# Softplus of an edge written as exponential and logarithm alone, with a bound on its argument found on the chip

## The chip, the cores and the metric

The kernel runs on one core of a Trainium2 chip. The time is that of the core from launch to the end of the program, in microseconds (us); of several runs the median counts. The engines are called as the profile calls them: PE (TensorE, with PEld for its weight loads), DVE (VectorE), ACT (ScalarE), POOL (GpSimd) and SP (SyncE, which here issues most DMAs).

## The reference

One layer of message passing on a graph of 6250 nodes and 200000 edges, 128 features. Of the nodes, h = relu(layernorm(x)) is multiplied by a weight matrix. An edge e goes from `dst[e]` to `src[e]` in the sense below; it has 20 attributes f in [0, 1) and a weight c in [0, 1):

```python
def shifted_softplus(x):
    return jax.nn.softplus(x) - LOG2

x = atomic_embedding @ W_in                              # h @ W_in
W_ij = shifted_softplus(f_ij @ W_f1 + b_f1) @ W_f2 + b_f2
W_ij = W_ij * f_ij_cutoff
x_ij = x[idx_j] * W_ij                                   # idx_j = dst
out = jax.ops.segment_sum(x_ij, idx_i, num_segments=N_ATOMS)   # idx_i = src
return shifted_softplus(out @ W_o1 + b_o1) @ W_o2 + b_o2
```

`W_f1` is 20x128, drawn from a normal distribution and divided by the root of 20; `b_f1` has a spread of 0.1. The argument of the edge's softplus is z = f @ W_f1 + b_f1. The result is added to the layer's input.

## The kernel before

**The edge work.** The edges stand in chunks of 128; 1563 chunks make 391 quads of four. One step i of the main loop works on several quads at once, each at another stage, and the order of every engine is written out by hand (`manual_schedule`): each step runs a fixed list of functions, and between them hooks put there beforehand by `at(step, point, function)`. The points are named after their engines (`D0`, `D1`, `DM`, `D2` for DVE, `A0` to `A2` for ACT, `PE2`, `L` for loads, `S` for scatters).

For a quad q the stages are:

- `s1_pe` (L309): z, a matmul of the attributes (split into three bf16 parts, 123 rows) into a PSUM bank of tag A. It is issued one step ahead.
- `s1_exp` and `s1_ln` on ACT: e = |z| (L314), e = exp(-e) (L315), e = ln(0.5 e + 0.5) (L320), each over 128x512.
- `s1_guard` on DVE (L485): a = max(z, 0) + e. This is softplus(z) - log 2.
- in the next step `s2_pe_x` and `s2_pe_w` on PE: the gathered node rows xg (L500, one-hot products), and W = b2 + a @ W_f2 (L497, L508, f32).
- `s2_copy` on ACT (L513): xc = xg times the edge weight, four instructions; `s2_m` on DVE (L523): the message m = W * xc.

**Where the messages go.** There are three ways. 168 quads are *sorted*: their messages are split into bf16 parts (L679), permuted into slots by products with one-hots (L665, L690), copied out by ACT (`mst`, L696), and later summed into the transposed accumulator `accT` by the *units*: 96 small products at a time (L784) into four PSUM banks, which DVE adds up (L795). What overflows the slots goes through L705 to L749 (`po`, `osum`, `os`) and a scatter. 192 quads are *listed*: their unsummed messages are scattered straight to DRAM by POOL, one instruction for each chunk (`scatter`, L585, an indirect DMA with addition), with duplicates sent to a dense list that is added later. 31 quads are plain: duplicates of a chunk are summed by a product (L535), and then scattered. There are four accumulators in DRAM, taken in turn.

**Tiles.** Four PSUM banks carry tag A (z, xg and W in turn), four tag B (all other products). The SBUF tags of the change: "e" with 2 buffers (e), "a" with 2 buffers (a; at the start also the first weights, `w1f`). Message tiles "s" have 4 buffers.

**Beside it.** The 49 blocks of attributes are split into bf16 parts 4096 edges at a time (`fb_1` to `fb_4`, L267 to L280, one block in eight steps), the node rows are prepared in 25 groups up to the middle of the loop (`prep_*`), and ranks for the sorted quads are counted in 21 groups (L596 to L654).

**The end.** What the fast path can't treat (an edge outside of its window, an overflow) is marked. A flag is computed and read into a register of every engine (L1233), and a loop over all chunks (L1234) runs as often as the flag says: 0 times, or once for each chunk. With a count of 0 all engines pass its branches, and its end waits for the landings of all DMAs. Then the tail loads the accumulators (L1309), sums them (L1315, L1321), and applies the output layers.

Of the kernel before, what the change touches and what calls it, by code (L numbers as in the profile page):

```python
# [7 lines left out]
F32 = mybir.dt.float32  # L8
BF16 = mybir.dt.bfloat16
# [11 lines left out]
P = 128  # L21
# [25 lines left out]
NACC = 4  # L47
FPARTS = ((0, 3), (3, 2), (5, 1))
CQ = 16
EARLY_N = 256  # L50


@with_exitstack
def tile_gnn(ctx: ExitStack, tc: tile.TileContext, x, fB, cT, srcT, srcr, dstr, win_, wf1, wf2, bias, bo1c, wo1,
# [64 lines left out]
    dropd = dp.tile([P, EP // P], BF16, name="dropd")  # L119

    con = cp.tile([P, 16], F32, name="con")
    loads = {}
    st = {}
    fst = {}
# [143 lines left out]
        fst[b]["f3"] = f3  # L268

    def fb_2(b):  # L270
        fr = wk.tile([P, FE], F32, tag="fr", name="fr", bufs=1)
        nc.vector.tensor_tensor(fr, fst[b]["f"], fst[b]["f3"][:, 0], op=ALU.subtract)
        fst[b]["fr"] = fr
# [36 lines left out]
        st.setdefault(q, {})["z"] = z  # L310

    def s1_exp(q):
        e = wk.tile([P, 512], F32, tag="e", name="e")
        nc.scalar.activation(e, st[q]["z"], AF.Abs)  # L314
        nc.scalar.activation(e, e, AF.Exp, scale=-1.0)  # L315
        st[q]["e"] = e

    def s1_ln(q):
        e = st[q]["e"]
        nc.scalar.activation(e, e, AF.Ln, bias=half, scale=0.5)  # L320
        st[q]["l"] = e

    def s1_oh(q):
        if q % 2 == 0:
# [151 lines left out]
    def l_ji(j):  # L476
# [2 lines left out]
        nc.vector.scalar_tensor_tensor(jd[:, 1:2], mp["L", j]["os"][:, P:P + 1], wgt2, jd[:, 0:1], op0=ALU.is_lt,  # L479
                                       op1=ALU.mult)  # L480
        mp["L", j]["jd"] = jd

    def s1_guard(q):
        a = wk.tile([P, 512], F32, tag="a", name="a")
        nc.vector.scalar_tensor_tensor(a, st[q]["z"], 0.0, st[q]["l"], op0=ALU.max, op1=ALU.add)  # L485
        st[q]["a"] = a

    def nchunks(q):
        return min(4, NCH - 4 * q)
# [349 lines left out]
    with tc.manual_schedule():  # L839
# [36 lines left out]
        nc.vector.tensor_scalar(thr, iot[:, 1:GRP], float(GN), None, op0=ALU.mult)  # L876

        def split3(dst, src, rows, c0, tag):
            p = wk.tile([rows, 3, P], BF16, tag="e", name=f"{tag}_parts")
            r = wk.tile([rows, P], F32, tag="xc", name=f"{tag}_rem")  # L880
            nc.vector.tensor_copy(p[:, 0], src)
            nc.vector.tensor_tensor(r, src, p[:, 0], op=ALU.subtract)
            nc.vector.tensor_copy(p[:, 1], r)
            nc.vector.tensor_tensor(p[:, 2], r, p[:, 1], op=ALU.subtract)
            nc.vector.tensor_scalar(dst, p[:, 0], con[:rows, c0:c0 + 1], None, op0=ALU.mult)
            for k in range(1, 3):
                nc.vector.scalar_tensor_tensor(dst, p[:, k], con[:rows, c0 + k:c0 + k + 1], dst, op0=ALU.mult,
                                               op1=ALU.add)
# [145 lines left out]
        def late_add():  # L1034
            nc.vector.tensor_tensor(bo2b, bo2b, late["bps"][:, 0], op=ALU.add)

        def r0_load(g):
            o, T = tgroups[g]
            t_ = ld.tile([P, 4, P], F32, tag="fb", name="r0t", bufs=2)
            nc.sync.dma_start(t_[:, :T], accs[0][o:o + T * P, :].rearrange("(t p) f -> p t f", p=P))  # L1040
            pst["r", g] = t_
# [14 lines left out]
        def x_bias(t):  # L1056
# [2 lines left out]
            nc.vector.tensor_tensor(v, v, bo2b.unsqueeze(1).to_broadcast([P, n, P]),  # L1059
                                    op=ALU.add)  # L1060

        at(mid, "L", late_loads)
        at(mid + 6 if spread else 0, "PE2", late_bias)
        at(mid + 7 if spread else 0, "D0", late_add)
# [104 lines left out]
        for i in range(max(NQ + 7, last + 16, r0_end + 2, lend + 24)):  # L1169
            if i % 2 == 0 and i // 2 + 2 <= (NQ - 1) // 2:  # L1170
                load_sc(i // 2 + 2)
            run(i, "L")
            run(i, "D0")
            if i < NQ:
                s1_oh(i)
            run(i, "D1")
            if 0 <= i - 1 < NQ:
                s1_eq(i - 1)
            if 0 <= i - 1 < NQ:
                s2_pe_x(i - 1)  # L1180
                s2_pe_w(i - 1)
            if i + 1 < NQ:
                s1_pe(i + 1)
            if i < NQ:
                s1_exp(i)
                s1_ln(i)
            if 0 <= i - 3 < NQ and not full[i - 1]:
                s3_copy(i - 3, 0)
                s3_copy(i - 3, 1)
            run(i, "A0")  # L1190
            if 0 <= i - 4 < NQ:
                s3_ji(i - 4)
            run(i, "A1")
            if 0 <= i - 1 < NQ:
                s2_copy(i - 1)
            if i < NQ:
                s1_guard(i)
            run(i, "DM")
            if 0 <= i - 1 < NQ:
                s2_m(i - 1)  # L1200
            if 0 <= i - 3 < NQ:
                s3_idx(i - 3)
            full[i] = sum(fn in banked for fn, _ in hooks.get((i, "PE2"), [])) > 2
            if 0 <= i - 2 < NQ:
                s3_pe(i - 2)
                if full[i]:
                    s3_copy(i - 2, 0)
                    s3_copy(i - 2, 1)
            run(i, "PE2")
            run(i, "A2")  # L1210
            run(i, "D2")
            if 0 <= i - 4 < NQ and plainq(i - 4):
                s3_scatter(i - 4)
            if 0 <= i - 2 < NQ and i - 2 not in mpi and not plainq(i - 2):
                s3_scatter(i - 2)
            run(i, "S")
# [10 lines left out]
    nc.tensor.matmul(fps[:, 6:7], onesc, dmax, start=True, stop=True)  # L1227
    flag1 = cp.tile([1, 1], F32, name="flag1")
    nc.vector.tensor_reduce(flag1, fps[:, 0:7], axis=AX.X, op=ALU.max)
    flagi = cp.tile([1, 1], I32, name="flagi")  # L1230
    nc.vector.tensor_scalar(flagi, flag1, 0.0, float(NCH), op0=ALU.is_gt, op1=ALU.mult)

    trips = nc.values_load(flagi, min_val=0, max_val=NCH, skip_runtime_bounds_check_because="0 or the number of chunks")  # L1233
    with tc.For_i(0, trips, 1) as ci:  # L1234
        dcol = wk.tile([P, 1], I32, bufs=1, tag="dcol", name="dcol")
        nc.sync.dma_start(dcol, dstr.rearrange("s (e o) -> (s e) o", o=1)[bass.ds(ci * P, P), :])
# [27 lines left out]
        nc.vector.tensor_scalar(ok[:, 0:1], rcol, float(WIN), None, op0=ALU.is_ge)  # L1264
        nc.vector.tensor_scalar(ok[:, 1:2], rcol, 0.0, None, op0=ALU.is_lt)
        nc.vector.tensor_tensor(ok[:, 2:3], ok[:, 0:1], ok[:, 1:2], op=ALU.add)
        nc.vector.scalar_tensor_tensor(ok[:, 3:4], ok[:, 2:3], xcol, ccol, op0=ALU.max, op1=ALU.mult)
        xw = wk.tile([P, P], F32, bufs=1, tag="rm", name="fxw")
        nc.vector.tensor_tensor(xw, x3[:, 0], x3[:, 1], op=ALU.add)
        nc.vector.tensor_tensor(xw, xw, x3[:, 2], op=ALU.add)  # L1270
        z = ps.tile([P, P], F32, tag="A", name="fz", bufs=4)
        nc.tensor.matmul(z, ws, ft[:K1, :], start=True, stop=True)
        e = wk.tile([P, P], F32, tag="e", name="fe")
        nc.scalar.activation(e, z, AF.Abs)
        nc.scalar.activation(e, e, AF.Exp, scale=-1.0)
        nc.scalar.activation(e, e, AF.Ln, bias=half, scale=0.5)
# [189 lines left out]
def _layout(inputs):  # L1466
    import numpy as np

    p = "L0_gnn_"
    x = np.asarray(inputs["x"])  # L1470
    src, dst = np.asarray(inputs["src"]), np.asarray(inputs["dst"])
    f, c = np.asarray(inputs["edge_attr_20"]), np.asarray(inputs["edge_weight1"])
    n, e = x.shape[0], src.shape[0]
    rb = f.shape[1]
    be = 4 * SC
    np_ = -(-n // P) * P
    ep = -(-e // be) * be
    pad = ep - e
    xp = np.pad(x, ((0, np_ - n), (0, 0)))
    fp = np.pad(f, ((0, pad), (0, 0)))  # L1480
    srcp = np.concatenate([src, (np.arange(pad) * (n // P) % n).astype(src.dtype)])
    dstp = np.pad(dst, (0, pad), mode="edge")
    n_sc = ep // SC
    caps = np.array(base_caps(np_, n_sc), np.float32)
    lane = np.arange(P)
    con = np.zeros((P, 16), np.float32)
    con[:, 0] = lane % HB // 3
    con[:, 1] = np.power(3.0, 63.0 - lane)
    con[:, 2] = 2.0 * con[:, 1]
    con[:, 3] = np_ + lane  # L1490
    con[:, 4] = 0.5
    con[:, 13] = lane
    con[:, 14] = np_ // GRP // 2 - con[:, 3]
    nch = -(-e // P)
    nq = -(-nch // 4)
    mq = sorted_quads(nq)
    order = [q for q in range(nq) if q not in mq] + mq + list(range(nq, ep // P // 4))
    cols = np.array([4 * q + c for q in order for c in range(4)])
    cmap = np.empty(ep // P, np.int32)
    cmap[cols] = np.arange(ep // P)  # L1500
    con[:n_sc // 2, 5] = caps[:n_sc // 2]
    con[:n_sc // 2, 6] = caps[n_sc // 2:]
    part = np.array([0, 0, 0, 1, 1, 2])
    for r in range(6 * rb + 3):
        con[r, 7 + (part[r // rb] if r < 6 * rb else r - 6 * rb)] = 1.0
    for r in range(3):
# [40 lines left out]
```

## Time and profile before

| | us |
|---|---|
| median of 3 runs (2149.01 to 2157.57) | 2155.19 |
| the profiled execution | 2165.61 |
| its span, first to last instruction | 2162.8 |
| mean granted PE clock | 0.963 |

The profile is one execution. Its page gives the busy time of each engine, and further views split it: by stretches of time (busy time of PE, PEld, DVE, ACT and POOL with the number of instructions in brackets, the granted clock, the mean busy share of the DMA engines and GB/s), by groups of instructions (line, engine, operation, output<-inputs, shape, count, then busy time, mean duration in ns, and the idle time of the engine just before, with what ended it), and by waits (who waited for what: total us, times, longest). In a timeline a row is the start, the length, the engine, the line, the operation, and in brackets the idle time before it. "issue" is idle time in which the engine waited for nothing that the profile shows.

The main loop runs from about 25 us (the first z) to about 2093 us; the last scatter starts at 2103.61 us and the first load of the tail at 2107.71 us.

### The profile page before, as it was taken

What the parts mean: (1) busy time and instruction counts of PE and PEld (TensorE: products, weight loads), DVE (VectorE), ACT (ScalarE), POOL (GpSimd) and SP (SyncE); (2) the same over time, 40 slices, a digit from 0 to 9 for tenths busy, and PEclk for the clock granted to TensorE, in tenths of its full rate; (3) what the DMA queues carried; (4) which work ended last, traced back from release to release, by engine and by line L of the source; (5) the groups of instructions that cost most, each with busy time, mean ns of one, the idle gap of its engine ahead of it and who ended that gap; (6) DMA issues with size and microseconds to landing.
All of it is one profiled execution on the core that took longest, in us unless ns stands there. A gap on an engine that the chain in (4) does not pass through costs nothing.

```text
span 2162.8 us, 58140 instructions
## 1 busy us (share of the span) xinstructions
PE 1889.9 (87%) x20377; PEld 1314.9 (61%) x20377; DVE 1846.0 (85%) x4782; ACT 1707.1 (79%) x4473; POOL 1635.6 (76%) x1040
## 2 busy tenths in 40 slices
PE   3578998988999899899999999899999999999966
PEld 2456665666666666566666666566666666666744
DVE  4689897997998999898989979989898898898845
ACT  3579887987887888788789878888888889888814
POOL 3678787877777777777777778878887888867674
PEclk8699999999999999999999999999999999999988
DMA  6887666766666666666666656666665666656648
GB/s 243 219 205 144 104 125 106 129 120 116 120 109 119 117 121 123 112 118 114 114 118 123 113 107 120 107 115 121 116 126 100 125 117 106 112 111 115 127 47 238
DMA packets 381191, 272.58 MB, mean 126 GB/s; under 512 B 97727, under 2 KB 341354, under 8 KB 380898
## 3 DMA queue, kind: packets, MB, share of 16 engines
q0 software_dynamic: 143728, 71.30, 33.0%
q1 hardware_dynamic: 236882, 197.50, 31.9%
q8 instruction: 160, 2.62, 0.5%
q14 instruction: 133, 1.09, 0.2%
q10 hardware_dynamic: 288, 0.07, 0.0%
HBM read 154.45 MB, written 114.24 MB: 124 GB/s over the span
## 4 chain that ended last, share of the span: by engine, by line
PE 44%; DVE 22%; ACT 17%; DMA 6%; issue 6%; POOL 3%; SPq 2%; DVEq 0%; ACTq 0%; POOLq 0%
PE pq L690 12%; PE un L784 11%; PE W L508 9%; ACT xc L513 4%; ACT e L315 3%; ACT e L314 3%; POOL acc L585 2%; DMA acc<-s,ji 2%; ACT mst L696 2%; DVE pm L665 2%; DVE eql L367 2%; DVE a L485 2%; DVE pt L679 2%; ACT e L320 2%; DVE accT L795 2%
## 5 line engine op out<-in xcount | busy, mean ns | idle before, releaser
L585 POOL DMA_INDIRECT acc<-s,lji x768 | 1238.7, 1613 | 343.1 <-issue 179.7
L690 PE MATMUL pq<-pt,pm 128*128 128x387 bf16 x2688 | 535.7, 342 | 48.2 <-DVE pt L679 23.0
L513 ACT ACTIVATE xc<-xg,cb 128x128 f32<-128x128 f32 x1564 | 446.0, 372 | 62.8 <-PE xg L500 54.8
L508 PE MATMUL W<-w,a 128*128 128x128 f32 x3128 | 466.4, 294 | 0.2 <-DVE a L485 0.2
L784 PE MATMUL un<-so,mst 32*128 32x392 bf16 x8064 | 385.5, 328 | 43.4 <-ACT os L749 27.1
L508 PEld LDWEIGHTS W<-w,a 128*128 128x128 f32 x3128 | 390.5, 196 | 42.5 <-issue 2.9
L690 PEld LDWEIGHTS <-pm 128*128 128x128 bf16 x2688 | 259.9, 99 | 242.1 <-issue 32.0
L696 ACT CAST mst<-pq 128x387 bf16<-128x387 f32 x672 | 297.9, 481 | 114.8 <-PE pq L690 82.4
L784 PEld LDWEIGHTS <-mst 32*128 32x128 bf16 x8064 | 250.0, 94 | 173.0 <-issue 92.6
L485 DVE SCALAR_TENSOR_TENSOR a<-z,e 128x512 f32<-128x512 f32 x391 | 266.2, 681 | 49.5 <-ACT e L320 41.9
L320 ACT ACTIVATE e<-e,con 128x512 f32<-128x512 f32 x391 | 282.3, 722 | 12.7
L585 POOL DMA_INDIRECT acc<-s,ji x123 | 201.5, 1638 | 99.3 <-ACT ji L566 43.5
L314 ACT ACTIVATE e<-z 128x512 f32<-128x512 f32 x391 | 239.7, 613 | 28.6 <-PE z L309 20.5
L315 ACT ACTIVATE e<-e 128x512 f32<-128x512 f32 x391 | 246.4, 630 | 12.4
L679 DVE TENSOR_TENSOR pt<-pt 128x512 f32<-128x512 f32 x336 | 231.8, 690 | 5.8
L665 DVE TENSOR_SCALAR pm<-iot,pos 128x576 bf16<-128x576 f16 x672 | 219.4, 387 | 0.0
L795 DVE TENSOR_TENSOR accT<-un,accT 128x392 f32<-128x392 f32 x320 | 158.7, 557 | 64.0 <-PE un L784 29.5
L769 DVE TENSOR_SCALAR so<-iot,mst 128x392 bf16<-128x392 f16 x672 | 188.6, 341 | 5.8 <-PE un L784 5.8
L309 PE MATMUL z<-ft,ws 123*128 123x512 bf16 x391 | 152.1, 390 | 32.1 <-DMA ft<-fsd 14.8
L585 POOL DMA_INDIRECT acc<-os,oji x96 | 154.0, 1604 | 31.1 <-issue 14.3
L523 DVE TENSOR_TENSOR s<-W,xc 128x512 f32<-128x512 f32 x192 | 131.5, 685 | 50.3 <-ACT xc L513 39.1
L500 PE MATMUL xg<-wn,oh 63*128 63x128 bf16 x1564 | 157.1, 222 | 13.4 <-DVE a L485 5.9
(197 smaller groups left out, 2662.0 us busy)
## 6 DMA issues: line engine op xcount, KB each, us to landing
rb<-reld SPq DMA_DIRECT2D x391, 64.0 KB
fsd<-f SPq DMA_DIRECT2D x49, 480.0 KB
ft<-fsd SPq DMA_DIRECT2D x195, 120.0 KB
sb<-src SPq DMA_DIRECT2D x169, 128.0 KB
fb<-in_fB_dram SPq DMA_DIRECT2D x49, 320.0 KB
ft<-fsd SPq DMA_DIRECT2D x195, 80.0 KB
wn<-tab SPq DMA_DIRECT2D x782, 15.8 KB
acc<-s,lji POOLq DMA_INDIRECT x768
```

The lines of the kernel that those rows point to most:

```text
L314: nc.scalar.activation(e, st[q]["z"], AF.Abs)
L315: nc.scalar.activation(e, e, AF.Exp, scale=-1.0)
L320: nc.scalar.activation(e, e, AF.Ln, bias=half, scale=0.5)
L485: nc.vector.scalar_tensor_tensor(a, st[q]["z"], 0.0, st[q]["l"], op0=ALU.max, op1=ALU.add)
L508: nc.tensor.matmul(W[:, c, :], st[q]["a"][:, c * P:(c + 1) * P], w2, start=False, stop=(c == 3))
L513: nc.scalar.mul(xc[:, c, :], st[q]["xg"][:, c, :], late["c", q // CQ][:, 4 * (q % CQ) + c:4 * (q % CQ) + c + 1])
L585: nc.gpsimd.indirect_dma_start(out=accs[k][:rows, :], out_offset=bass.IndirectOffsetOnAxis(ap=ji, axis=0), in_=s, in_offset=None, compute_ ...
L665: nc.vector.tensor_scalar(pm[:, c], iot[:, :SLOTS], rk[r]["pos"][:, 4 * j + c:4 * j + c + 1], None, op0=ALU.is_equal)
L679: nc.vector.tensor_tensor(pt[:, :, k * P:(k + 1) * P], a, high(a), op=ALU.subtract)
L690: nc.tensor.matmul(t[:, :PW], mp[q]["pm"][:, c, s * P:(s + 1) * P], high(mp[q]["pt"][:, c:c + 1, :PW])[:, 0], start=(c == 0), stop=(c == 3))
L696: nc.scalar.copy(mp[q]["ms", s][:, :PW], mp[q].pop(("q", s))[:, :PW])
L784: nc.tensor.matmul(ts[g][:, :GN], mp[q]["ms", s][v, k * P:(k + 1) * P], mp[q]["oh"][v], start=(q == qs[0] and k == 0), stop=(q == qs[-1] a ...
```

## The change

The softplus of an edge is computed as ln(0.5 exp(z) + 0.5), without |z| and without max(z, 0): Abs on ACT and the guard on DVE are left out, and the product with W_f2 reads what ACT wrote. This is right as long as exp(z) stays in range. So a bound on |z| is found on the chip: the largest magnitude of the attributes (one reduction for each of the 49 blocks, in `fb_2`) or 1, times the largest column sum of |W_f1| and |b_f1|. If it is over 60, a new loop before the old one clears the accumulators, and the old one treats every chunk, with the old formula.

```diff
+ZMAX = 60.0
...
+    fmax = cp.tile([P, NB], F32, name="fmax")
+    zcol = cp.tile([P, 4], F32, name="zcol")
...
     def fb_2(b):
+        nc.vector.tensor_reduce(fmax[:, b:b + 1], fst[b]["f"], axis=AX.X, op=ALU.max, apply_absolute_value=True)
...
     def s1_exp(q):
-        e = wk.tile([P, 512], F32, tag="e", name="e")
-        nc.scalar.activation(e, st[q]["z"], AF.Abs)
-        nc.scalar.activation(e, e, AF.Exp, scale=-1.0)
-        st[q]["e"] = e
+        a = wk.tile([P, 512], F32, tag="e", name="a", bufs=3)
+        nc.scalar.activation(a, st[q]["z"], AF.Exp)
+        st[q]["a"] = a
 
     def s1_ln(q):
-        e = st[q]["e"]
-        nc.scalar.activation(e, e, AF.Ln, bias=half, scale=0.5)
-        st[q]["l"] = e
+        a = st[q]["a"]
+        nc.scalar.activation(a, a, AF.Ln, bias=half, scale=0.5)
...
-    def s1_guard(q):
-        a = wk.tile([P, 512], F32, tag="a", name="a")
-        nc.vector.scalar_tensor_tensor(a, st[q]["z"], 0.0, st[q]["l"], op0=ALU.max, op1=ALU.add)
-        st[q]["a"] = a
...
+        def bound_abs():
+            t_ = wk.tile([K1, P], F32, tag="h", name="wabs", bufs=1)
+            nc.scalar.activation(t_, w1f, AF.Abs)
+            v_ = wk.tile([K1, P], F32, tag="rm", name="wsel", bufs=1)
+            nc.vector.tensor_copy(v_, con[:K1, 15:16].to_broadcast([K1, P]))
...
+        def bound_sum():
+            t_ = ps.tile([P, 512], F32, tag="B", name="gps", bufs=4)
+            nc.tensor.matmul(t_[:, :P], late["wabs"][1], late["wabs"][0], start=True, stop=True)
...
+        def bound_max():
+            nc.vector.tensor_reduce(zcol[:, 0:1], late["gps"][:, :P], axis=AX.X, op=ALU.max)
+
+        def large_own():
+            nc.vector.tensor_reduce(zcol[:, 1:2], fmax, axis=AX.X, op=ALU.max)
+            nc.vector.scalar_tensor_tensor(zcol[:, 1:2], zcol[:, 1:2], 1.0, zcol[:, 0:1], op0=ALU.max, op1=ALU.mult)
+            nc.vector.tensor_scalar(zcol[:, 2:3], zcol[:, 1:2], ZMAX, None, op0=ALU.is_gt)
+
+        def large_any():
+            t_ = ps.tile([P, 512], F32, tag="B", name="lps", bufs=4)
+            nc.tensor.matmul(t_[:, 0:1], onesf, zcol[:, 2:3], start=True, stop=True)
...
+        def large_all():
+            nc.vector.tensor_scalar(zcol[:, 3:4], late["lps"][:, 0:1], 0.0, None, op0=ALU.is_gt)
...
+            k = clear(mid + 9, busy, 2)
+            at(k - 1, "D2", bound_abs)
+            at(k, "PE2", bound_sum)
+            at(k + 1, "D0", bound_max)
+            k = clear(NQ - 1, busy, 2)
+            at(k - 1, "D2", large_own)
+            at(k, "PE2", large_any)
+            at(k + 1, "D0", large_all)
...
-            if i < NQ:
-                s1_guard(i)
...
+    nc.vector.tensor_tensor(flag1, flag1, zcol[0:1, 3:4], op=ALU.max)
+    flagi = cp.tile([1, 2], I32, name="flagi")
+    nc.vector.tensor_scalar(flagi[:, 0:1], flag1, 0.0, float(NCH), op0=ALU.is_gt, op1=ALU.mult)
+    nc.vector.tensor_copy(flagi[:, 1:2], zcol[0:1, 3:4])
+
+    anew = nc.values_load(flagi[:, 1:2], min_val=0, max_val=1, skip_runtime_bounds_check_because="0 or 1")
+    with tc.For_i(0, anew, 1):
+        nc.vector.memset(accT, 0.0)
+        for k in range(1, NACC):
+            for j in range(ZR):
+                zero_piece(nc.sync, k, j)
```

The first group of the bound stands in the middle of the loop (step 209), the second at its end (step 396). In the loop over the chunks, which keeps the old formula, the tile of e gets tag "a".

More of the change, by code (lines that the diff above doesn't have):

```diff
@@ L878, in split3 @@
         def split3(dst, src, rows, c0, tag):
-            p = wk.tile([rows, 3, P], BF16, tag="e", name=f"{tag}_parts")
+            p = wk.tile([rows, 3, P], BF16, tag="e", name=f"{tag}_parts", bufs=3)
             r = wk.tile([rows, P], F32, tag="xc", name=f"{tag}_rem")
@@ L1035, in late_add @@
             nc.vector.tensor_tensor(bo2b, bo2b, late["bps"][:, 0], op=ALU.add)
+        def bound_abs():
[3 more added lines that the diff above has]
+            nc.vector.tensor_copy(v_, con[:K1, 15:16].to_broadcast([K1, P]))
+            late["wabs"] = t_, v_
+        def bound_sum():
+            t_ = ps.tile([P, 512], F32, tag="B", name="gps", bufs=4)
+            nc.tensor.matmul(t_[:, :P], late["wabs"][1], late["wabs"][0], start=True, stop=True)
+            late["gps"] = t_
+        def bound_max():
[7 more added lines that the diff above has]
+            nc.tensor.matmul(t_[:, 0:1], onesf, zcol[:, 2:3], start=True, stop=True)
+            late["lps"] = t_
+        def large_all():
+            nc.vector.tensor_scalar(zcol[:, 3:4], late["lps"][:, 0:1], 0.0, None, op0=ALU.is_gt)
         def r0_load(g):
@@ L1060, in x_bias @@
                                     op=ALU.add)
+        if spread:
+            k = clear(mid + 9, busy, 2)
[6 more added lines that the diff above has]
+            at(k + 1, "D0", large_all)
+        else:
+            for fn in (bound_abs, bound_sum, bound_max):
+                at(0, "D0", fn)
+            for fn in (large_own, large_any, large_all):
+                at(NQ + 1, "D0", fn)
         at(mid, "L", late_loads)
@@ L1229, in tile_gnn @@
     nc.vector.tensor_reduce(flag1, fps[:, 0:7], axis=AX.X, op=ALU.max)
-    flagi = cp.tile([1, 1], I32, name="flagi")
-    nc.vector.tensor_scalar(flagi, flag1, 0.0, float(NCH), op0=ALU.is_gt, op1=ALU.mult)
-    trips = nc.values_load(flagi, min_val=0, max_val=NCH, skip_runtime_bounds_check_because="0 or the number of chunks")
+    nc.vector.tensor_tensor(flag1, flag1, zcol[0:1, 3:4], op=ALU.max)
[8 more added lines that the diff above has]
+                zero_piece(nc.sync, k, j)
+    trips = nc.values_load(flagi[:, 0:1], min_val=0, max_val=NCH,
+                           skip_runtime_bounds_check_because="0 or the number of chunks")
     with tc.For_i(0, trips, 1) as ci:
@@ L1266, in tile_gnn @@
         nc.vector.tensor_tensor(ok[:, 2:3], ok[:, 0:1], ok[:, 1:2], op=ALU.add)
+        nc.vector.tensor_tensor(ok[:, 2:3], ok[:, 2:3], zcol[:, 3:4], op=ALU.max)
         nc.vector.scalar_tensor_tensor(ok[:, 3:4], ok[:, 2:3], xcol, ccol, op0=ALU.max, op1=ALU.mult)
@@ L1272, in tile_gnn @@
         nc.tensor.matmul(z, ws, ft[:K1, :], start=True, stop=True)
-        e = wk.tile([P, P], F32, tag="e", name="fe")
+        e = wk.tile([P, P], F32, tag="a", name="fe")
         nc.scalar.activation(e, z, AF.Abs)
@@ L1493, in _layout @@
     con[:, 14] = np_ // GRP // 2 - con[:, 3]
+    con[:6 * rb, 15] = 1.0 / 6
+    con[6 * rb:6 * rb + 3, 15] = 1.0 / 3
     nch = -(-e // P)
```

## The prediction

> **What bounds the kernel now.** I read the page's first two parts, then busy time by stretches, then the timeline of a few steps of the main loop, then the waits of TensorE (PE) and GpSimd (POOL), and last the end of the loop.
>
> ```profile
> span 2162.8 us, 58140 instructions
> ...
> PE 1889.9 (87%) x20377; PEld 1314.9 (61%) x20377; DVE 1846.0 (85%) x4782; ACT 1707.1 (79%) x4473; POOL 1635.6 (76%) x1040
> ```
>
> No engine stands out in these shares of the span. By stretches (microseconds from the start; busy time of PE, weight loads, VectorE (DVE), ScalarE (ACT), POOL; granted clock, DMA share) it is clearer:
>
> ```profile
> 200.00:1800.00 1600.00, 1460.77 (x16249) 1007.74 (x16247) 1442.14 (x3790) 1325.31 (x3484) 1253.84 (x778) 0.98 0.64 116
> 1800.00:2060.00 260.00, 246.32 (x2672) 175.60 (x2672) 216.87 (x530) 227.97 (x611) 195.54 (x124) 1.00 0.64 117
> 0.00:200.00 200.00, 120.07 (x853) 88.39 (x854) 137.50 (x360) 122.88 (x320) 124.36 (x96) 0.86 0.78 206
> ```
> ```profile
> 1800.00:2000.00 200.00, 192.27 (x2087) 134.86 (x2084) 170.34 (x420) 177.27 (x472) 153.71 (x97) 1.00 0.64 115
> ```
>
> From 200 to 1800 us PE is busy 1460.77/1600 = 91%, DVE 90%, ACT 83%. From 1800 to 2000 us the node preparation is over and DVE is down to 170.34/200 = 85%: PE rises to 192.27/200 = 96%, although ACT is busier there (89%). So PE is held back in the long stretch by something that DVE and ACT do late. The timeline shows it. PE first, then ACT, around the same steps (start, length, engine, line):
>
> ```profile
> 1284.61 0.38 PE L309 MATMUL z<-ft,ws 123*128 123x512 bf16 x1
> ...
> 1288.69 0.38 PE L309 MATMUL z<-ft,ws 123*128 123x512 bf16 x1
> 1289.05 5.19 PE L784 MATMUL un<-so,mst 32*128 32x392 bf16 x96
> ...
> 1295.49 0.38 PE L309 MATMUL z<-ft,ws 123*128 123x512 bf16 x1
> ```
> ```profile
> 1286.80 0.63 ACT L314 ACTIVATE e<-z 128x512 f32<-128x512 f32 x1
> 1287.46 0.63 ACT L315 ACTIVATE e<-e 128x512 f32<-128x512 f32 x1
> 1288.12 0.72 ACT L320 ACTIVATE e<-e,con 128x512 f32<-128x512 f32 x1
> 1288.75 0.25 ACT L749 COPY os<-osum 128x132 f32<-128x132 f32 x1
> 1288.90 0.87 ACT L696 CAST mst<-pq 128x387 bf16<-128x387 f32 x2
> ```
>
> The chain that ended last, in order of time, has other groups of the same 96 (start, length):
>
> ```profile
> 200.38 4.15 PE un L784 x96
> ```
>
> One step of the loop is 4.08 us (z at 1284.61 to z at 1288.69), PE without a break; the next, with the 96 unit products, takes 6.80 us. Those 96 took 5.19 us here; without a wait it is 4.15. The difference of 1.04 us is a wait for banks that ACT must empty (os, mst), and ACT gets there only after Abs, Exp and Ln. The waits of PE and POOL from 200 to 2000 us (total, times, longest):
>
> ```profile
> PE un L784 <- ACT os L749: 26.5, 30, 7.1
> PE pq L690 <- DVE pt L679: 18.4, 25, 1.4
> PE pq L690 <- DVE rt L654: 10.1, 7, 1.9
> ```
> ```profile
> POOL acc L585 <- issue: 197.4, 646, 0.5
> POOL acc L585 <- DVE s L523: 83.4, 38, 7.5
> POOL acc L585 <- DVE bn L183: 35.0, 14, 8.0
> POOL acc L585 <- ACT ji L566: 17.0, 5, 9.4
> ```
>
> PE waits for ACT and DVE. POOL, which scatters the messages, is the second thing to see. Each scatter is followed by an "issue" gap of 197.4/646 = 0.305 us. So 778 scatters of 200 to 1800 us occupy 1253.84 + 778 × 0.305 = 1491 us of 1600, 93%; only the rest is waiting for DVE's products. POOL is therefore a floor just under PE: whatever is won, the stretch can't fall under about 1491 us.
>
> **The change, part by part.**
>
> ```profile
> L585 POOL DMA_INDIRECT acc<-s,lji x768 | 1238.7, 1613 | 343.1 <-issue 179.7 <-DVE s L523 83.4 <-DVE bn L183 35.0
> L485 DVE SCALAR_TENSOR_TENSOR a<-z,e 128x512 f32<-128x512 f32 x391 | 266.2, 681 | 49.5 <-ACT e L320 41.9 <-issue 4.0 <-ACT e L315 3.5
> L314 ACT ACTIVATE e<-z 128x512 f32<-128x512 f32 x391 | 239.7, 613 | 28.6 <-PE z L309 20.5 <-issue 0.2
> L315 ACT ACTIVATE e<-e 128x512 f32<-128x512 f32 x391 | 246.4, 630 | 12.4
> L272 DVE TENSOR_TENSOR fr<-fb,f 128x640 f32<-128x640 f32 x49 | 40.1, 819 | 3.3 <-ACT f L267 3.3
> L633 DVE TENSOR_REDUCE rank<-pr 128x32 f32<-128x512 f32 x21 | 14.4, 686 | 0.7
> ```
>
> *Abs goes.* 391 × 613 ns = 239.7 us off ACT. The Exp that stays reads the bank itself, as Abs did; between 613 ns (Abs from a bank) and 630 ns (Exp from SBUF) I count it unchanged.
>
> *The guard (max and add) goes.* 391 × 681 ns = 266.2 us off DVE. Its wait for Ln goes too, which held everything queued behind it on DVE (the product of the step before, its one-hots, the evacuation of the units). The W product on PE now waits for Ln directly. It stands one step later in PE's order, and needs no earlier product than before, so nothing new is late. The argument's bank is also free after Exp instead of after the guard.
>
> *The bound on the argument comes in.* 49 maxima over 128x640 on DVE. No reduction of that size is in the trace: 686 ns for 512 elements scales to 858, the 640-element subtraction took 819. I take 0.84 us, 49 × 0.84 = 41 us, one in about eight steps, and keep 0.8 to 0.9. DVE's net is 266 − 41 = 225 us less. The one before the first product could lie on the start-up path: +1 us. The products and small reductions of the bound (two matmuls, some ten small operations in all) come once per run, on engines that the guard and Abs have just relieved by more: nothing. SP's queue gets only the zeroing inside a loop that isn't entered.
>
> *The third buffer and the moved tags* add no wait: step i takes the buffer of step i − 3, whose product PE finished in step i − 2.
>
> *A second conditional loop stands before the tail.* Its trip count is 0. This comes after the last scatter, where no other work hides it:
>
> ```profile
> 2101.76 1.54 POOL L585 DMA_INDIRECT acc<-s,ji  x1 [0.31 <-issue]
> 2103.61 1.54 POOL L585 DMA_INDIRECT acc<-os,oji  x1 [0.30 <-issue]
> ```
> ```profile
> 2092.29 1.51 DVE L795 TENSOR_TENSOR accT<-un,accT 128x392 f32<-128x392 f32 x3 [5.76 <-PE un L784]
> ```
> ```profile
> L1234 POOLq COMPARE_BRANCH  x3: 38/41/53, 2101.9 to 2107.8; - x3
> L1234 POOLq INC_SWDGE_SEM  x1: 1153/1153/1153, 2102.1 to 2102.1; - x1
> ```
> ```profile
> L1233 POOLq TENSOR_LOAD <-flagi x1: 494/494/494, 2101.3 to 2101.3; - x1
> ```
>
> The one loop of before took POOL's queue from 2101.3 (0.49 us load of the count) over 1.15 us to branches that end at 2107.8, part of it under the last scatters. The new loop passes under them in its place, and this one follows behind the last landing: load 0.5, queue mark 1.15, branches and semaphores about 1. I take 3 us, between 1 (only the load and branch show) and 6 (all of 2101.3 to 2107.8 again). The flag now needs the end of DVE's loop work, 2093.8 us by the row above, where the scatters run on to 2105.2: hidden by them. If that cover is gone it costs what DVE ends later.
>
> **The sum.** From 200 to 1800 us DVE loses 1600/2163 of 225 us, about 166, and ACT about 177. At today's length that is DVE (1442 − 166)/1600 = 80% and ACT 72%, both under what they are in the stretch 1800 to 2000, where PE reached 96%. At 96% the 1460.8 us of PE take 1520 us: −80. POOL's 1491 us would then be 98% of the stretch; a stream that is still fed in bursts will not quite get there, so I take −72. From 1800 to 2060 us PE is at 246.32/260 = 95% already: −4. The first 200 us wait for loads and landings (DMA share 0.78): 0. Start +1, second loop +3. Sum −72 us. The profiled execution took 2165.6 us, 10.4 above the median of 2155.2; I take the difference from the median: **2083 us**. This case's own range, with PE between 94.5% and 97.5% in the stretch (1546 and 1498 us, so −54 and −102) and the bounds of the loop: 2055 to 2110.
>
> **The rivals.**
>
> *A new wait takes the place of the old.* The waits that name ACT os or the guard go, but the in-order evacuations behind pt, rt and mst stay, because a rank group or a node group puts DVE over PE in its steps anyway. For it: 18.4 + 10.1 us of PE's waits name other DVE work. Against it: those queues too start 0.68 us a step earlier. Then only the units' wait is saved, 26.5 us by its row, and the loop and the start cost 4: −22, 2133, between 2115 and 2150.
>
> *More than forecast: PE is not the limit at all.* If PE's busy time hides slack, the stretch falls until POOL's 1491 us stop it: −109, and −4 at the end, +4: 2046, between 2030 and 2055. The row for it is weight loads at 61%; against it, steps such as the one of 4.08 us, where one matmul group starts as the other ends. The Trainium skill, "Perfetto Trace Analysis", section Identifying the Most-Contended Engine, says that matmul busy time is a bad measure of how near PE is to its limit, and that weight-load share or useful work should be used; by that rule PE at 61% has room, DVE at 85% is the contended engine, and this rival is the likelier one. The gap-free steps of this trace speak against it.
>
> *Slower: the scatters stretch.* The other scatters, and the first of all in the timeline:
>
> ```profile
> L585 POOL DMA_INDIRECT acc<-s,ji x123 | 201.5, 1638 | 99.3 <-ACT ji L566 43.5 <-issue 27.1 <-DMA acc<-s,ji 20.5
> L585 POOL DMA_INDIRECT acc<-os,oji x96 | 154.0, 1604 | 31.1 <-issue 14.3 <-ACT mst L696 4.9 <-ACT e L314 2.4
> ```
> ```profile
> 55.90 1.78 POOL L585 DMA_INDIRECT acc<-s,ji  x1 [18.47 <-ACT ji L566]
> ```
>
> POOL's 768 + 123 + 96 = 987 scatters take 1594.2/987 + 0.305 = 1.92 us each, and run from 55.9 to 2105.2 us. Packed closer, they meet the loads and each other in the DMA queues (share 0.64), and each must follow the last one on its accumulator. From 2049/987 = 2.08 us a scatter on they alone last as long as the loop does now; at 2.13 us the run takes 987 × 0.05 = 50 us more: 2205. Against it: in the drain at the end they stand at 1.85 us apart with no wait.
>
> *It doesn't do what it says.* If the bound came out over 60, the loop over 1563 chunks would run, for milliseconds. The bound is the sum of 20 weights' magnitudes (spread 0.22) and a bias, times a feature of at most 1: about 5. Not expected.
>
> **How the numbers follow.** Forecast 0.60; new wait 0.20, of which 0.06 lies within 0.5% of before (2144 to 2166; about what a measurement of this kernel can tell from no change); more than forecast 0.13; slower 0.06; not what it says 0.01. Faster by over 0.5%: 0.60 + 0.14 + 0.13 = 0.87; same 0.06; slower 0.07. The range reaches down into the case of more (2045) and up through half of the new wait (2130).
>
> **What would show it.** Right: no Abs and no guard rows; Exp of 391 at 0.6 us; the maxima at 0.84 us; PE at 95 to 97% between 200 and 1750 us; unit groups of 96 nearly all at 4.1 us; POOL's wait for DVE's product under 40 us; DVE and ACT near 75% and 70% of the span; 3 us more between the last scatter and the first tail load. Wrong: PE still at 92% with waits for other DVE lines (first rival), POOL without waits and PE well under 95% of busy time in the stretch (the floor was nearer than I put it), or scatters over 1.7 us on average (the slower case).

## The result, and the profile after

The changed kernel takes 2076.2 us (median of 4 runs, 2069.40 to 2079.35) against 2153.45 us of the kernel before beside it: ratio 0.9637, 95% interval 0.9605 to 0.967, so 77 us less. Forecast were 2083 us and 72 us less. The profiled execution is the fastest of the four (2069.40 us), that of before lay 10 us over its median; the two profiled spans are therefore 95 us apart, some 18 us more than the medians. The line numbers of the main loop are 3 smaller than before (z is L313, Exp L318, Ln L323).

The page's first part, of the changed kernel:

```profile
span 2067.6 us, 57535 instructions
...
PE 1854.7 (90%) x20381; PEld 1285.7 (62%) x20381; DVE 1657.1 (80%) x4448; ACT 1490.1 (72%) x4083; POOL 1631.5 (79%) x1040
```

DVE lost 189 us of busy time and ACT 217; PE lost 35 with the same work. By stretches (same columns as before):

```profile
200.00:1730.00 1530.00, 1438.38 (x16307) 987.64 (x16304) 1299.43 (x3538) 1161.59 (x3193) 1258.26 (x782) 0.98 0.68 122
1730.00:1920.00 190.00, 188.89 (x2108) 133.97 (x2108) 152.06 (x390) 155.39 (x436) 157.80 (x98) 1.00 0.69 123
```

The 16307 matmuls of the first row took 1530 us, where 16249 took 1600 us before. The same piece of the loop can be cut out by its quads. These are the z of quads 28 and 338, before and then after:

```profile
195.91 0.38 PE L309 MATMUL z<-ft,ws 123*128 123x512 bf16 x1
1795.58 0.38 PE L309 MATMUL z<-ft,ws 123*128 123x512 bf16 x1
```
```profile
191.20 0.38 PE L313 MATMUL z<-ft,ws 123*128 123x512 bf16 x1
1713.36 0.38 PE L313 MATMUL z<-ft,ws 123*128 123x512 bf16 x1
```

The piece took 1599.7 us before and takes 1522.2 now. So 77 of the 95 us between these two executions lie here. From there to the last z 15 us were won (259.5 to 244.2), and 5 us ahead of quad 28; the end of the program takes 2 us more. A second profile of the changed kernel (the repeat below) ends only 78 us before that of the kernel before, about as far as the medians are apart. In it the same piece takes 1535.6 us: 64 us less, with 13 behind it and 3 ahead.

PE is at 1438.38/1530 = 94% in the first stretch, up from 91%, DVE at 85% and ACT at 76%. In the second, behind the node preparation, PE is at 188.89/190 = 99%, where it was at 95% before. What PE and POOL wait for between 200 and 1730 us (total, times, longest):

```profile
PE un L781 <- ACT os L746: 19.0, 3, 14.2
PE pq L687 <- DVE pt L676: 8.5, 14, 1.3
...
PE pq L687 <- DVE rt L651: 6.3, 6, 1.7
```
```profile
POOL acc L582 <- issue: 179.7, 588, 0.6
POOL acc L582 <- DVE s L520: 24.7, 19, 3.0
POOL acc L582 <- DMA acc<-s,lji: 23.1, 64, 1.6
POOL acc L582 <- DVE bn L186: 10.9, 7, 2.2
```

In the same window of the kernel before, the units waited for ACT and POOL for DVE's products:

```profile
PE un L784 <- ACT os L749: 24.3, 27, 7.1
```
```profile
POOL acc L585 <- DVE s L523: 78.7, 33, 7.5
```

Of the 27 waits of the units for ACT three are left, but one of these lasts 14 us, of which more below; in total they fell only from 24.3 to 19.0 us. POOL's waits for DVE's products fell from 78.7 to 24.7 us. With its issue gaps of 179.7/588 = 0.306 us, POOL is now occupied for 1258.26 + 782 × 0.306 = 1497 of 1530 us, 98%. A step of the kind that the prediction showed, with 96 unit products, at about the same time but 14 quads later in the loop, on PE's timeline:

```profile
1285.55 0.38 PE L313 MATMUL z<-ft,ws 123*128 123x512 bf16 x1
...
1285.87 4.45 PE L781 MATMUL un<-so,mst 32*128 32x392 bf16 x96
...
1291.57 0.38 PE L313 MATMUL z<-ft,ws 123*128 123x512 bf16 x1
```

It takes 6.02 us (z at 1285.55 to z at 1291.57) instead of 6.80, since the 96 products wait 0.3 us for their banks and not 1.04. Over all 84 groups, from the first product's start to the last one's end, the median fell from 5.11 to 4.45 us; 36 of them last under 4.3 us (21 before) and 16 over 5 us (52 before). At the end of the loop, POOL and SP of the changed kernel (last scatter, first load of the tail):

```profile
2006.32 1.54 POOL L582 DMA_INDIRECT acc<-os,oji  x1 [0.30 <-issue]
```
```profile
2013.35 3.06 SPq L1356 DMA_DIRECT2D ta_in<-acc  x5
```

From the start of the last scatter to the first load there are now 7.03 us, against 2107.71 − 2103.61 = 4.10 before. In four later profiles with two loops it is 6.88 to 7.01.

### The profile page after: what moved, and what is told of

It reads as the page before. It is cut to its first block, busy times and chain, and to the rows that moved or that the text cites. A ratio compares the mean times of both kernels' runs of the same rounds, so it can differ in the third digit from the quotient of the medians.

```text
span 2067.6 us, 57535 instructions
## 1 busy us (share of the span) xinstructions
PE 1854.7 (90%) x20381; PEld 1285.7 (62%) x20381; DVE 1657.1 (80%) x4448; ACT 1490.1 (72%) x4083; POOL 1631.5 (79%) x1040
## 5 line engine op out<-in xcount | busy, mean ns | idle before, releaser
L687 PE MATMUL pq<-pt,pm 128*128 128x387 bf16 x2688 | 527.9, 339 | 27.0 <-DVE pt L676 10.7
L781 PE MATMUL un<-so,mst 32*128 32x392 bf16 x8064 | 378.3, 331 | 31.9 <-ACT os L746 19.3
L693 ACT CAST mst<-pq 128x387 bf16<-128x387 f32 x672 | 303.1, 481 | 132.6 <-PE pq L687 130.0
L781 PEld LDWEIGHTS <-mst 32*128 32x128 bf16 x8064 | 228.4, 94 | 175.0 <-issue 70.0
L323 ACT ACTIVATE a<-a,con 128x512 f32<-128x512 f32 x391 | 282.3, 722 | 12.7
L582 POOL DMA_INDIRECT acc<-s,ji x123 | 197.0, 1602 | 82.8 <-issue 25.9
L318 ACT ACTIVATE a<-z 128x512 f32<-128x512 f32 x391 | 237.4, 607 | 33.2 <-PE z L313 17.4
L313 PE MATMUL z<-ft,ws 123*128 123x512 bf16 x391 | 151.6, 388 | 16.1 <-POOL b2rep L927 9.3
L494 PE MATMUL W<-b2rep,onesb 64*128 64x512 bf16 x391 | 153.8, 393 | 0.0
L520 DVE TENSOR_TENSOR pt<-W,xc 128x512 f32<-128x512 f32 x168 | 115.2, 686 | 34.9 <-ACT xc L510 29.4
```

The source lines that it names most:

```text
L318: nc.scalar.activation(a, st[q]["z"], AF.Exp)
L323: nc.scalar.activation(a, a, AF.Ln, bias=half, scale=0.5)
L520: nc.vector.tensor_tensor(m[:, :, :P], st[q]["W"], st[q]["xc"], op=ALU.mult)
L582: nc.gpsimd.indirect_dma_start(out=accs[k][:rows, :], out_offset=bass.IndirectOffsetOnAxis(ap=ji, axis=0), in_=s, in_offset=None, compute_ ...
L687: nc.tensor.matmul(t[:, :PW], mp[q]["pm"][:, c, s * P:(s + 1) * P], high(mp[q]["pt"][:, c:c + 1, :PW])[:, 0], start=(c == 0), stop=(c == 3))
L693: nc.scalar.copy(mp[q]["ms", s][:, :PW], mp[q].pop(("q", s))[:, :PW])
```

## The experiments

The theory: PE was held back because ACT and DVE were both full and reached its banks and inputs late, and POOL's scatters stand close behind PE as the next limit. The rivals: that the way from z to a counts, or one engine alone; that POOL is no limit; that it was one before. All ratios are to the kernel before the change, run beside.

**Abs back on ACT.** The guard stays away.

```diff
         a = wk.tile([P, 512], F32, tag="e", name="a", bufs=3)
+        nc.scalar.activation(a, st[q]["z"], AF.Abs)
         nc.scalar.activation(a, st[q]["z"], AF.Exp)
```

> The changed kernel with Abs put back on ACT ahead of Exp (its result is overwritten, so the output is the same); the guard stays away. Theory 'occupancy' (ACT and DVE reached PE's banks and products late because they were full): ACT gains 391 x 0.61 = 240 us of work, 2076 becomes about 2105 (2095 to 2120), and the wait of the unit products for ACT's copy of osum comes back. Rival 'path' (what counted was the time from z to a): the path is 0.61 of the 1.3 us longer again that were won, so about half of the 77 us, 2110. Rival 'DVE alone' (ACT had slack, the guard was the whole of it): under 10 us, 2076 to 2086.

Measured: 2129.96 us, ratio 0.9899 (0.9881 to 0.9918). The waits of PE in this run, 200 to 1730 us:

```profile
PE un L782 <- ACT os L747: 22.1, 34, 2.7
PE po L703 <- ACT h L224: 17.9, 15, 2.3
PE pq L688 <- DVE pt L677: 13.6, 20, 1.4
```

54 us come back, more than any theory said, and with them the wait of the units for ACT, 34 times. "DVE alone" falls: without the guard but with Abs only 1.0% of the 3.6% is won. "Occupancy" and "path" foresaw nearly the same time for this run, so it doesn't separate them.

**An instruction like the guard, beside the path.**

```diff
+    def s1_guard(q):
+        g = wk.tile([P, 512], BF16, tag="gd", name="g", bufs=1)
+        nc.vector.scalar_tensor_tensor(g, st[q]["z"], 0.0, st[q]["a"], op0=ALU.mult, op1=ALU.add)
...
+            if i < NQ:
+                s1_guard(i)
             run(i, "DM")
```

> The changed kernel with an instruction on DVE of the guard's inputs, place and length whose result nobody reads (the product with W_f2 still waits for ACT's Ln). Theory 'occupancy': DVE has 391 x 0.68 = 266 us of work again, 2076 becomes about 2105 (2095 to 2125). Rival 'path': nothing on the way from z to a changes, 2076 within 8 us. Rival 'ACT alone': as the path, under 10 us.

Measured: 2124.25 us, ratio 0.9887 (0.9863 to 0.991). PE's waits, 200 to 1730 us:

```profile
PE pq L691 <- DVE pt L680: 21.6, 23, 1.7
...
PE pq L691 <- DVE rt L655: 11.6, 7, 2.5
PE un L785 <- DVE pr L631: 11.5, 9, 1.8
```

The first part of its page:

```profile
PE 1879.8 (89%) x20381; PEld 1294.2 (61%) x20381; DVE 1877.2 (89%) x4839; ACT 1492.8 (70%) x4083; POOL 1630.4 (77%) x1040
```

48 us come back although the product never waits for this instruction. Now the waits name DVE's work, and the units' wait for ACT (os) is down to 2.7 us in 2 waits: each of the two runs brings back mainly its own engine's waits. "ACT alone" and "path" fall. "Occupancy" is here more than the 0.68 us of work. The instruction reads z and what Ln wrote, so with the work come back the guard's wait for Ln on DVE and the longer hold on the bank of z:

```profile
DVE g L487 <- ACT a L323: 26.9, 11, 6.9
```

How the 48 us divide between the work, this wait and the bank was not tested.

Both runs still contain what the change added. The 54 and 48 us that come back make 102 us, more than the net win of 77 us. They are close to the win before these additions: 77, plus the 18 us that the maxima cost (below) and the 3 us of the second loop, is 98 us. So if the maxima cost the same in these runs, each engine's relief is worth about half of the win, and the two simply add up; nothing here shows that one needs the other.

**The same on the path.**

```diff
+    def s1_guard(q):
+        a = st[q]["a"]
+        nc.vector.scalar_tensor_tensor(a, st[q]["z"], 0.0, a, op0=ALU.mult, op1=ALU.add)
```

> As the run before it, but the instruction writes a in place, so that the product with W_f2 waits for DVE again; the value added is zero times z, so the output is the same. Theory 'occupancy': as the run with the guard beside the path, within 8 us of it (about 2108), since the product stands one step later in PE's order. Rival 'path': clearly later than that run, by 20 us or more, about 2110 where that run stays at 2076.

Measured: 2130.06 us, ratio 0.9913 (0.9887 to 0.9938). That is 6 us over the run beside the path, with overlapping intervals: on DVE the path itself is worth little or nothing. For Abs it was not tested apart.

**Fewer scatters, after and before.**

```diff
             w, k = divmod(plain[q] - LB, SW)
-            for c in range(nchunks(q)):
+            for c in range(nchunks(q) - 1):
```

> The changed kernel without the scatter of the fourth chunk of each listed quad (those messages are left out of the sum): 192 of 987 scatters, 192 x 1.92 = 369 us of POOL's 1890. Theory 'POOL is the floor now' (its scatters and their gaps fill 98% of the stretch from 200 to 1730 us): the time falls by 30 to 50 us, to about 2036, until PE at 96 to 97% stops it. Rival 'PE and its waits are still the limit': only the drain behind the last product goes, 2 to 12 us, 2064 to 2074.

Measured: 2059.06 us, ratio 0.957 (0.9552 to 0.9588); 14 us less by the ratios, 17 by the medians. It falls short of what the theory said, and a little over what the rival allowed: POOL is not the only limit. In this run the units' waits for ACT (os) are also down to 0.6 us from 19.0; how much of the gain is POOL's time and how much these waits stays open.

> The kernel before the change, without the scatter of the fourth chunk of each listed quad (those messages are left out of the sum). Theory 'POOL was not the limit before' (93% of the stretch, the rest of it waits for DVE's products): only the drain at the end gets shorter, 0 to 15 us less, 2138 to 2153. Rival 'POOL held the loop before, too': 17 us or more less, as in the changed kernel.

Measured: 2152.9 us, ratio 0.9998 (0.9983 to 1.0014). Before the change POOL was no limit that a measurement within about 4 us can show; even the shorter drain didn't show.

**Fewer products for PE, alone and with fewer scatters.**

```diff
-            for k in range(3):
+            for k in range(2):
                 for g in range(4):
...
-                                     start=(q == qs[0] and k == 0), stop=(q == qs[-1] and k == 2))
+                                     start=(q == qs[0] and k == 0), stop=(q == qs[-1] and k == 1))
```

> The changed kernel with two of the three bf16 parts in the unit products (the lowest part of the sorted messages is left out): 64 instead of 96 products in each of 84 groups, 84 x 32 x 0.043 = 115 us less for PE. Theory 'two limits side by side' (PE with what it waits for, and POOL at 98% just under it): only 20 to 40 us of it show, 2036 to 2056, and POOL has no gap left. Rival 'PE alone': 80 us or more, under 1996. Rival 'neither, the order of DVE and ACT': under 10 us.

Measured: 2053.44 us, ratio 0.9542 (0.9522 to 0.9562): 23 us less than the changed kernel by the medians, 20 by the ratios, of the 115 us that PE has less to do. The stretch from 200 to 1730 us of this run:

```profile
200.00:1730.00 1530.00, 1392.99 (x14281) 946.83 (x14280) 1312.03 (x3576) 1177.91 (x3237) 1276.85 (x788) 0.97 0.69 123
```

PE is down to 91% and POOL has 1276.85 + 788 × 0.306 = 1518 of 1530 us: POOL is full. PE feels it through the overflow rows, whose buffers the scatters free:

```profile
PE un L781 <- ACT os L746: 29.2, 5, 15.9
```

The granted clock is 0.97 in this stretch, 0.98 in that of the changed kernel; what that cost was not separated.

> The changed kernel with both: two of three parts in the units, and without the scatter of the fourth chunk of each listed quad (both are left out of the sum). Theory 'two limits side by side': the gain is more than the sum of the two alone (17 us for the scatters alone, 20 to 40 for the units alone): 70 to 110 us, 1966 to 2006. Rival 'PE alone': as the run with fewer units. Rival 'neither': under 30 us.

Measured: 2010.66 us, ratio 0.9332 (0.9313 to 0.935): 66 us less, where the two alone gave 17 and 23 (14 and 20 by the ratios). So after the change PE and POOL limit the loop side by side; what one of them gives up, the other takes. The gain is a little under the theory's 70 us. The stretch and POOL's waits in this run:

```profile
200.00:1730.00 1530.00, 1423.04 (x14725) 969.31 (x14723) 1339.64 (x3681) 1213.32 (x3340) 1031.88 (x637) 0.98 0.63 119
```
```profile
POOL acc L582 <- DVE s L520: 208.7, 76, 10.7
```

POOL waits for products again, and PE is at 93% with DVE at 88%: then PE with its waits for DVE probably holds the loop again; no run tests it.

**Without the maxima, and with the maxima at another place.**

```diff
     def fb_2(b):
-        nc.vector.tensor_reduce(fmax[:, b:b + 1], fst[b]["f"], axis=AX.X, op=ALU.max, apply_absolute_value=True)
...
         def large_own():
-            nc.vector.tensor_reduce(zcol[:, 1:2], fmax, axis=AX.X, op=ALU.max)
-            nc.vector.scalar_tensor_tensor(zcol[:, 1:2], zcol[:, 1:2], 1.0, zcol[:, 0:1], op0=ALU.max, op1=ALU.mult)
+            nc.vector.tensor_copy(zcol[:, 1:2], zcol[:, 0:1])
```

> The changed kernel without the 49 maxima over the attributes (the bound is then that of the weights alone, which is the same for these inputs). Theory 'DVE's work still counts a little': 41 us less for DVE, at the rate of the run with the guard beside the path (48 us of time for 266 of work) 7 us, 2064 to 2074. Rival 'hidden': within 3 us of 2076.

Measured: 2058.06 us, ratio 0.9549 (0.9525 to 0.9573). 18 us less by the medians, 0.9 ± 0.4% by the ratios: the maxima are not hidden, and seem to cost more for each microsecond of DVE's time (18 us for 41) than the guard did (48 us for 266). ACT's waits name a possible reason: its second cast of a block stands behind the maximum on DVE. The row of the changed kernel (whole run), and that of the next experiment, which has the maxima behind the last subtraction of the block:

```profile
ACT f L280 <- DVE fr L276: 17.6, 25, 1.2
```
```profile
ACT f L279 <- DVE fr L275: 3.8, 8, 0.8
```

The next four runs were made on another chip, where the kernel before took 2164.68 us. The first of them is the changed kernel again:

> The changed kernel itself, timed beside the three that follow, since steps of some 10 us are to be told apart. Both theories: 2076 within 6 us.

Measured: 2086.32 us, ratio 0.9624 (0.9598 to 0.965): within its interval the ratio of the first time, though 2076 within 6 us was missed.

```diff
     def fb_4(b):
...
+        nc.vector.tensor_reduce(fmax[:, b:b + 1], fst[b]["f"], axis=AX.X, op=ALU.max, apply_absolute_value=True)
         del fst[b]
```

> The changed kernel with each of the 49 maxima moved on DVE from ahead of the subtraction that ACT waits for (fb_2) to behind the last subtraction of the block (fb_4), one step later; the same work. Theory 'place' (without the maxima the time fell by 18 us, more than 41 us of DVE's work explains at the rate of the guard, because ACT's second cast waits behind each maximum: 12.9 us in 19 waits against 2.3 in 8): 8 to 18 us less than the changed kernel beside it, about 2064. Rival 'amount' (it is DVE's work as such): within 4 us of it.

Measured: 2078.38 us, ratio 0.9599 (0.9574 to 0.9624), 8 us less than the changed kernel beside it, with overlapping intervals. ACT's wait is down by 14 us (the rows above). So part of the maxima's price may be their place; how the 18 us divide between place and amount stays open.

**More buffers for the overflow rows.**

```diff
-        s = sp_.tile([P, 132], F32, tag="os", name="os", bufs=2)
+        s = sp_.tile([P, 132], F32, tag="os", name="os", bufs=4)
...
-        ji = sp_.tile([P, 1], I32, tag="oji", name="oji", bufs=2)
+        ji = sp_.tile([P, 1], I32, tag="oji", name="oji", bufs=4)
```

The first edit stands in both copies of these rows. It goes after the one long wait of the changed kernel, on the timelines of ACT, POOL and PE:

```profile
346.75 0.72 ACT L323 ACTIVATE a<-a,con 128x512 f32<-128x512 f32 x1
361.25 0.27 ACT L746 COPY os<-osum 128x132 f32<-128x132 f32 x1 [13.77 <-DMA acc<-os,oji]
```
```profile
331.62 1.54 POOL L582 DMA_INDIRECT acc<-os,oji  x1 [0.31 <-DMA acc<-s,lji]
...
357.94 1.54 POOL L582 DMA_INDIRECT acc<-os,oji  x1 [0.30 <-issue]
```
```profile
361.56 1.82 PE L781 MATMUL un<-so,mst 32*128 32x392 bf16 x20 [14.18 <-ACT os L746]
```

ACT stands still from 347.5 to 361.25 us, because the copy of new overflow rows needs a buffer whose scatter (357.94) is queued on POOL behind the scatters of listed messages; PE stands behind ACT.

> The changed kernel with 4 buffers in place of 2 for the overflow rows (os) and their indices, which the scatters free. Theory 'POOL's lag reaches ACT' (a wait of 13.8 us of ACT for the landing of a scatter of os, and 14.2 us of PE behind it): 5 to 14 us less, 2062 to 2071. Rival 'the lag is only moved, since POOL is at 98%': within 4 us.

Measured: 2066.19 us, ratio 0.9531 (0.9509 to 0.9554), 20 us less than the changed kernel beside it, more than the one wait. The waits of ACT for scatters of os are gone from this run, and what PE waits for os is:

```profile
PE un L781 <- ACT os L746: 1.3, 4, 0.4
```

The lag was not only moved, but taken up: POOL's waits for DVE's products between 200 and 1730 us are 14.4 us, where the changed kernel beside it has 26.4. With the same scatters and the same products as before this wins as much as 369 us less for POOL or 115 us less for PE did. So a part of what tied PE to POOL was these two buffers.

**All three together**, with one outer conditional loop around both others:

```diff
-    flagi = cp.tile([1, 2], I32, name="flagi")
+    flagi = cp.tile([1, 3], I32, name="flagi")
...
+    nc.vector.tensor_scalar(flagi[:, 2:3], flag1, 0.0, None, op0=ALU.is_gt)
+    some = nc.values_load(flagi[:, 2:3], min_val=0, max_val=1, skip_runtime_bounds_check_because="0 or 1")
+    with tc.For_i(0, some, 1):
         anew = nc.values_load(flagi[:, 1:2], min_val=0, max_val=1, skip_runtime_bounds_check_because="0 or 1")
         with tc.For_i(0, anew, 1):
...
         trips = nc.values_load(flagi[:, 0:1], min_val=0, max_val=NCH,
```

> A version for both: the maxima behind, 4 buffers for the overflow rows, and one outer conditional loop around the clearing and the chunks, so that with a count of 0 the engines pass one loop instead of two before the tail. Theory: the sum of the two runs before it and 2.8 us of the loop, 2045 to 2062, and 4.1 us from the last scatter's start to the first load of the tail instead of 7.0. Rival 'one limit hides the other' (POOL at 99% stops whatever the buffers and places win): 2060 to 2070, the loop's 3 us alone in full.

Measured: 2063.53 us, ratio 0.9518 (0.9496 to 0.9541): 23 us less than the changed kernel beside it, and 3 less than with the buffers alone. It beats the kernel before the change and the changed one. The stretch from 200 to 1730 us, the last scatter and the first load of the tail:

```profile
200.00:1730.00 1530.00, 1452.74 (x16442) 996.19 (x16438) 1306.09 (x3562) 1167.66 (x3223) 1274.40 (x788) 0.99 0.69 123
```
```profile
1999.45 1.54 POOL L582 DMA_INDIRECT acc<-os,oji  x1 [0.30 <-issue]
```
```profile
2003.61 12.04 SPq L1360 DMA_DIRECT2D ta_in<-acc  x15
```

From the last scatter to the first load there are 4.16 us: the 2.9 us of the second loop are gone. On top of the buffers no more than that shows, but the intervals overlap. POOL stands at 1274.40 + 788 × 0.306 = 1516 of 1530 us, 99%, which fits the rival: the place of the maxima can't show any more. It isn't decided. The three gains alone would add up to 20 + 8 + 3 = 31 us, 23 came, and each is known within some 5 us.

## Why the prediction was right

- **Both engines made PE late: shown.** Each part undone alone brings back mainly the waits of its own engine, and 48 to 54 us. That only 1.0 to 1.1% of the 3.6% is left in these runs does not mean that the two parts need each other: the runs also pay for the maxima and the second loop, and without these costs each part would be worth about half of the win, by the sum above. The prediction did not split the gain between the parts; it read PE's 96% off a stretch in which DVE was lighter and ACT busier than before it.
- **The sizes of the parts.** Exp from a bank takes 607 ns (counted 613 to 630), a maximum 810 ns (counted 840):

```profile
L318 ACT ACTIVATE a<-z 128x512 f32<-128x512 f32 x391 | 237.4, 607 | 33.2 <-PE z L313 17.4
L274 DVE TENSOR_REDUCE fmax<-fb 128x1 f32<-128x640 f32 x49 | 39.7, 810 | 0.0
```

  DVE's busy time fell by 189 us and not by 225, ACT's by 217 and not by 240. Durations can overlap with those of their neighbours: in the prediction's timeline of ACT, Ln starts at 1288.12 and takes 0.72 us, but the next copy starts at 1288.75. With the guard beside the path DVE's busy time was 1877.2 us, so 391 × 0.68 = 266 us of guard are worth 220 of busy time. DVE therefore stayed at 80% of the span, where 75% was expected.
- **The stretch at 96% of PE: near, and the total partly by luck.** −72 was forecast for the stretch and −4 + 1 + 3 = 0 for everything else. By quads the stretch gave −77 in the one pair of profiles, which is 18 us too far apart, and −64 in the other. PE reached 94% and not 96%, but its busy time for the same work fell too; waits of the unit products for their banks count as busy in part (of the 1.04 us too many in the group of 5.19 us only 0.13 are idle time in the trace), so some of that fall can be such waits. Behind the stretch PE went from 95% to 99%, which gave 13 to 15 us and not 4, and the start gave 3 to 5 where nothing was forecast. So a stretch that may have given less than its −72, in which the maxima took 18 us, and other parts that gave more than forecast add up to 77. That 2083 lies so near to 2076 is in part luck.
- **The sign "unit groups of 96 nearly all at 4.1 us": not met.** 36 of 84 are, within 0.2 us.
- **POOL just under PE: right, and nearer than I put it.** At 98% POOL limits the loop beside PE, as the runs with fewer scatters and fewer products show. The rival "PE is not the limit at all" was half right: taking 115 us from PE alone won 23. The rule of the Trainium skill that it named ("Perfetto Trace Analysis", Identifying the Most-Contended Engine) would have had DVE, with its 85%, as the limit of the kernel before. The runs decide otherwise: those with the guard's work put back relieve ACT alone, with the maxima on DVE besides, and still win 0.9 to 1.1% over the kernel before.
- **The price of the maxima: too low.** They cost about 18 us (0.9 ± 0.4%), where the sum only took their 41 us off DVE's gain and had no term of time for them.
- **The second loop at 3 us: right**, 7.03 − 4.10 = 2.9, and gone in the last run.
- **The range.** Its terms give 2051 (−102 − 4 + 1 + 1) to 2104 (−54 − 4 + 1 + 6), not 2055 to 2110. The result lies in both.
- **What the prediction did not see:** a small wait grew, at another place than the first rival's. With the loop faster, POOL's lag reached the two buffers of the overflow rows (ACT waited 6.4 us for them before, 18.2 after), and through ACT also PE; with two more, 20 us were to be had.

## What to carry to other kernels

Where two engines are both nearly full, relieving one can show little: PE and POOL alone gave 23 and 17 us here, both together 66. Undo each part of a change alone before judging it, and count what the change added for its own sake: two parts that each seem to leave little of the gain can still simply add up. Work out the occupied time of the engine that only scatters, with its gaps, before anything else gets faster: it is the floor of the next step, and a small pool of buffers that it frees can then stop an engine that has nothing to do with it. Small work that is added ahead of an instruction for which another engine waits may cost more than the same work elsewhere; here the place alone is not proven.

## What the runs showed of the hardware

An untaken conditional loop over all engines, passed behind the last landing, took 2.9 us here; inside another untaken loop it is not passed at all, and the 4.16 us are those of one loop (4.10 before). In the drain of the kernel before, POOL's scatters of 128 rows stood 1.85 us apart (1.54 busy, 0.30 of gap). Those of the lists took 1.613 us in the mean before and 1.611 after:

```profile
L582 POOL DMA_INDIRECT acc<-s,lji x768 | 1237.3, 1611 | 266.9 <-issue 184.6 <-DVE s L520 25.0 <-DMA acc<-s,lji 22.0
```

The loop was about 4% shorter, and yet the scatters did not stretch: the rival on the slower side falls.
